# A graph kernel on one core: edges to the first 256 destination nodes taken from SBUF, the others gathered

## The chip, the cores and the metric

The kernel runs on one core of one Trainium2 chip. The time of a run is the device time of that core in microseconds (us), here the median of three runs. Beside the runs there is one profiled execution, from which every duration comes. A core has five engines, each with its own queue that it works off in order: TensorE (PE, its weight loads are shown as PEld), VectorE (DVE), ScalarE (ACT), GpSimd (POOL) and SyncE (SP, which issues DMAs).

## The reference

There are 12500 nodes with 256 features and 200000 edges from `src` to `dst`. `src` is uniform; `dst` is 12500 times the square of a uniform number, so low nodes are hit far more often. The edges come sorted by `dst`.

```python
h = relu(layernorm(x));  e = h @ W_P_w + W_P_b + W_pos          # 12500 x 128
for each of 2 layers:                                            # 8 heads of 16
    q = e[src] @ qT;  k = e[dst] @ kT;  v = e[dst] @ vT          # one row per edge
    a = exp(clip(sum over a head of q * k, -10, 10))
    agg = segment_sum(a * v, src) / (segment_sum(a, src) + 1e-8)
    e = layernorm(agg + e) * ln_s + ln_b
x = x + e @ inv_w + inv_b
h = relu(layernorm(x))
x = x + segment_sum(edge_weight * (h @ w_nbr)[src], dst) + h @ w_own + bias
```

## The kernel before

Nodes are taken in 98 tiles of 128. An edge belongs to the tile of its `src` (in the two attention layers) or of its `dst` (in the neighbour sum at the end). Edges are laid out in columns of 128, one edge to a partition, and the columns of a tile follow one another, filled up with idle edges; in the code `MAIN` = 1616 columns hold all edges of the drawn inputs.

**Prelude.** `sort_edges` (L306) makes one 32-bit key of each edge, with the tile in the high bits, the place of `src` within its tile (or 128 for a filler) from bit 14 and `dst` below, counts the edges of each tile (`count_tiles`, L175, by one-hot planes that TensorE multiplies), adds fillers and sorts 128 x 2048 keys by a bitonic network on VectorE (`stage`, L267). It leaves `idx_a` (the `dst` of each edge), `place_a` (its place within the tile), the same places as rows in DRAM (`place_d`) and the tile of each column (`near_d`). Beside it `embed` (L543) makes the first embedding of every tile and `project` (L510) its q, which stays in SBUF, and its rows of k and v, 256 floats a node, which go to the DRAM table `tkv`. `plan_as_they_come` (L394) lays out the neighbour sum. The flags in `bad` choose, at L1111, between a general arm and `short_arm` (L1007), which the drawn inputs take.

**Attention.** `short_attention` (L825) goes over 202 steps of `K2` = 8 columns for each layer. In its steady order, for step t:
- `gathers(t+2)`: 8 indirect DMAs from GpSimd's queue (L848, issued at L581) fetch the k and v rows of 8 columns into `kvg`, which has three buffers. An indirect DMA takes one column: 128 rows of 1 KB.
- `spread_hot(t+2)`: ScalarE turns the places, which a DMA has spread over the partitions (`load`, L837), into transposed one-hot matrices by Abs and Relu (L855, L857).
- `take_q(t+1)`: TensorE multiplies them with the tile's q (L871), which gives each edge its q in PSUM. The tile is a register that `registers` loads.
- `logits(t)`: VectorE multiplies q and k (L879), sums each head (L881), clips (L882). `exps(t)`: ScalarE's Exp (L887) and a copy (L888).
- `edge_hot(t+1)`: the one-hot matrix of places (L893). `weighted(t)`: VectorE scales v (L898).
- `sums(t)`: TensorE multiplies the one-hot matrix with the weights and the scaled v (L910) and adds up two steps in one PSUM tile `ps` of two windows, cleared by a product with zeros (L903); `add_window` (L590) adds it to `acc` every second step.

The order inside this arm is written out by hand (`manual_schedule`); L918 to L948 give it. Node work of finished tiles is hung into it at slots: `attended_later` (L685) divides, adds and normalises, `next_layer` (L733) projects for layer two, and after layer two `neighbour_rows` (L758) makes the rows of `h @ w_nbr` and the own part. The step from which a tile may be finished comes from `ends_by` (L80), a bound on the columns used by the first tiles (16.5 a tile).

**Neighbours.** `short_neighbours` (L950) gathers 1616 columns of the table `th` and sums them with weighted one-hot matrices (L604). `results` stores the output.

Of the kernel before, what the change touches and what calls it, by code (L numbers as in the profile page):

```python
# [33 lines left out]
P = 128  # L35
# [18 lines left out]

CG = -(-NCOL // P)
# [10 lines left out]
BASE = 1 << 29  # L66
TILE_MASK = 127 << 22
LAST = BASE | NT << 22 | P << 14

HI, LO, CB = -(-NT // 8), 8, 9  # L70
HPARTS = 6
# [4 lines left out]
MOST = RC - 1  # L76
SLOPE, SLACK = 16.5, 8.0


def ends_by(t):  # L80
    return min(MAIN, int(SLOPE * (t + 1) + SLACK))
# [3 lines left out]
def gnn_kernel(ctx, tc, x, src, dst, edge_weight, wp_w, wp_b, w_pos, q1, k1, v1, ln1_s, ln1_b,  # L85
# [23 lines left out]
    part_neg = const.tile([P, 1], F32, name="part_neg")  # L109
    nc.vector.tensor_scalar(part_neg, part_f, -1.0, None, op0=OP.mult)  # L110
    bad = const.tile([P, 4], F32, name="bad")
# [26 lines left out]
    def qkv_of(pool, layer):  # L138
        t = pool.tile([P, 3, D], F32, name=f"qkv{layer}")
        for j, w in enumerate(((q1, k1, v1), (q2, k2, v2))[layer]):  # L140
# [3 lines left out]
    qkv_sb = [None, qkv_of(const, 1)]  # L144
    ln_sb = [(row(s, D, f"lns{i}"), row(b, D, f"lnb{i}"))
             for i, (s, b) in enumerate(((ln1_s, ln1_b), (ln2_s, ln2_b)))]
# [7 lines left out]

    near_d = [dram.tile([1, CG * P // RC, RN], I32, name=f"near{i}") for i in range(2)]

# [4 lines left out]
    idx_a = keep.tile([P, NCOL], I32, name="idx_a")  # L161

    place_a = keep.tile([P, NCOL], F32, name="place_a")
# [11 lines left out]
    def count_tiles(pool, psum, key, shift, room):  # L175


        cross = psum.tile([P, CB * LO], F32, name="small", tag="turned")
        nb = HC // CB

        planes = [r.bitcast(BF16)[:, 0:n * HC] for r, n in zip(room, (HI, LO))]
        for part in range(HPARTS):
            have = min(HC, EC - part * HC)
            ti = pool.tile([P, HC], I32, name="ti")
            if have < HC:
                nc.vector.memset(ti, 127)
            nc.vector.tensor_scalar(ti[:, 0:have], key[:, part * HC:part * HC + have], shift, 127,
                                    op0=OP.logical_shift_right, op1=OP.bitwise_and)
            for n, down, mask, hot in ((HI, 3, 15, planes[0]), (LO, 0, 7, planes[1])):
                digit = pool.tile([P, HC], I32, name="digit")  # L190
                nc.vector.tensor_scalar(digit, ti, down, mask, op0=OP.logical_shift_right, op1=OP.bitwise_and)
                short = pool.tile([P, HC], BF16, name="short")
                nc.vector.tensor_copy(short, digit)
                for i in range(n):
                    nc.vector.tensor_scalar(hot[:, i * HC:(i + 1) * HC], short, float(i), None, op0=OP.is_equal)
            for c in range(nb):
                nc.tensor.matmul(cross[:CB * HI], planes[0][:, c::nb], planes[1][:, c::nb],
                                 start=(part == 0 and c == 0), stop=(part == HPARTS - 1 and c == nb - 1))
            yield
# [3 lines left out]
        own = pool.tile([P, LO, CB], F32, name="own")  # L203
        nc.vector.tensor_mul(own[:CB * HI], cross[:CB * HI].rearrange("p (l c) -> p l c", c=CB),
                             same[:CB * HI, None, :].to_broadcast([CB * HI, LO, CB]))
        sums = pool.tile([P, LO], F32, name="sums")
        nc.vector.tensor_reduce(sums[:CB * HI], own[:CB * HI], AX.X, OP.add)
# [5 lines left out]
        by_tile = psum.tile([P, CB * LO], F32, name="small", tag="turned")  # L213
        nc.tensor.matmul(by_tile[:HI * LO, 0:LO], wide[:CB * HI].rearrange("p h l -> p (h l)"), sums[:CB * HI],
                         start=True, stop=True)

        low = pool.tile([P, 1], I32, name="low")
        nc.vector.tensor_scalar(low, part_i, LO - 1, None, op0=OP.bitwise_and)
        low_f = pool.tile([P, 1], F32, name="low_f")
        nc.vector.tensor_copy(low_f, low)  # L220
        pick = pool.tile([P, LO], F32, name="pick")
        nc.vector.tensor_scalar(pick, iota_f[:, 0:LO], low_f, None, op0=OP.is_equal)
        nc.vector.tensor_mul(pick[:HI * LO], pick[:HI * LO], by_tile[:HI * LO, 0:LO])
        n = pool.tile([P, 1], F32, name="n")
        nc.vector.memset(n, 0.0)
        nc.vector.tensor_reduce(n[:HI * LO], pick[:HI * LO], AX.X, OP.add)
        return n

    def columns_of(pool, psum, n, which):
# [5 lines left out]
        nc.vector.tensor_scalar(cols, ni, float(LEAST), None, op0=OP.max)  # L235
# [4 lines left out]
        nc.vector.tensor_scalar(bad[:NT, which:which + 1], ends[:NT], float(MAIN), None, op0=OP.is_gt)  # L240
        if which == 0:
            by = pool.tile([P, 1], F32, name="by")
            nc.vector.tensor_scalar(by, part_f, SLOPE, SLOPE + SLACK, op0=OP.mult, op1=OP.add)
            late = pool.tile([P, 1], F32, name="late")
            nc.vector.tensor_tensor(late[:NT], ends[:NT], by[:NT], op=OP.is_gt)
            few = pool.tile([P, 1], F32, name="few")
            nc.vector.tensor_scalar(few[:NT - 1], cols[:NT - 1], float(MOST), None, op0=OP.is_lt)
            nc.vector.tensor_tensor(late[:NT - 1], late[:NT - 1], few[:NT - 1], op=OP.add)
            nc.vector.tensor_copy(bad[:NT, 3:4], late[:NT])
        return cols, ends  # L250

    def fillers(pool, dest, wide, n, cols):

        want = pool.tile([P, 1], F32, name="want")
        nc.vector.tensor_scalar(want, cols, float(P), n, op0=OP.mult, op1=OP.subtract)
        mask = wide.bitcast(I32)[:, 0:FILL]
        for k in range(LEAST):
            left = pool.tile([P, 1], F32, name="left")
            nc.vector.tensor_scalar(left, want, float(k * P), None, op0=OP.subtract)
            nc.vector.tensor_scalar(mask[:, k * P:(k + 1) * P], iota_f, left, None, op0=OP.is_lt)  # L260
        key = pool.tile([P, 1], I32, name="fkey")
        nc.vector.tensor_scalar(key, part_i, 22, None, op0=OP.logical_shift_left)
        nc.vector.tensor_scalar(key, key, BASE | P << 14, None, op0=OP.bitwise_or)
        nc.vector.memset(dest, LAST)
        nc.vector.copy_predicated(dest[:NT], mask[:NT], key[:NT].to_broadcast([NT, FILL]))
# [40 lines left out]
    def sort_edges(pool, psum, mine, other, weight=None):  # L306

        which = 0 if weight is None else 1
# [12 lines left out]
        yield  # L321
        nc.vector.tensor_tensor(ai[:, 0:EC], ai[:, 0:EC], bi[:, 0:EC], op=OP.bitwise_or)
# [4 lines left out]
        n = yield from count_tiles(pool, psum, ai[:, 0:EC], 22, (b, w))  # L327
        cols, _ = columns_of(pool, psum, n, which)
        fillers(pool, ai[:, FILL0:W], b, n, cols)
# [40 lines left out]
        yield from turned(psum, a, b, NCOL)  # L370
        ai, bi = a.bitcast(I32)[:, 0:NCOL], b.bitcast(I32)[:, 0:NCOL]
        if w is None:
            nc.vector.tensor_scalar(idx_a, bi, (1 << 14) - 1, None, op0=OP.bitwise_and)
            nc.vector.tensor_scalar(wi[:, 0:NCOL], bi, 14, 255, op0=OP.logical_shift_right, op1=OP.bitwise_and)
            nc.vector.tensor_copy(place_a, wi[:, 0:NCOL])
# [13 lines left out]
        nc.vector.tensor_scalar(ai[0:1], ai[0:1], NT - 1, None, op0=OP.min)  # L389
        near = near_d[which][:, 0:NCOL // RC, :]  # L390
# [3 lines left out]
    def plan_as_they_come(pool, psum):  # L394
# [15 lines left out]
        cols, ends = columns_of(pool, psum, n, 1)  # L410
# [201 lines left out]
    def attention_edges(pool, psum, q, acc, layer, chunks):  # L612
        for ch in chunks:
# [8 lines left out]
            for g in range(0, RC, K2):  # L622
                kvg = pool.tile([P, K2, 2 * D], F32, name="kvg", bufs=3)
                for k in range(K2):
                    c = ch * RC + g + k
                    gather(kvg[:, k, :], tkv[layer], idx_a[:, c:c + 1])

                far = pool.tile([P, K2 * P], BF16, name="far", bufs=2)
                nc.scalar.activation(far, spread[:, g * P:(g + K2) * P], AF.Abs, bias=part_neg)
# [55 lines left out]
    def attended_later(node, slots, acc, t0, t, layer):  # L685
# [4 lines left out]
        def load():  # L690
            e = tiles["e"] = node.tile([P, D], F32, name="e", bufs=4)
            nc.sync.dma_start(e[:n], emb_d[layer][t * P:t * P + n, :])

        def whole():
# [5 lines left out]
            y = node.tile([P, D], F32, name="y")  # L700
# [23 lines left out]
        def copy_e():  # L724
            et = tiles["et"] = node.tile([P, P], F32, name="et")
# [32 lines left out]
    def neighbour_rows(node, slots, weights, acc, acc1, t0, t):  # L758

        n = rows_of(t)  # L760
        inv_sb, w2_sb, inv_b_row, bias_row = weights
# [6 lines left out]
        def outwards():  # L768
            po = tiles["po"] = slots["psum"].tile([P, 4 * P], F32, name="out_e", tag="n1")
            nc.tensor.matmul(po[:n, 0:GD], tiles["et"][:, :n], inv_sb, start=True, stop=False)  # L770
            nc.tensor.matmul(po[:n, 0:GD], ones[0:1, :n], inv_b_row, start=False, stop=True)
# [15 lines left out]
        def centred():  # L787
            c = tiles["c"] = node.tile([P, GD], F32, name="c")
# [7 lines left out]
        def relu():  # L796
            ht = tiles["ht"] = node.tile([P, 2, P], F32, name="ht")
            nc.scalar.activation(ht[:, :, :n], tiles["pt2"][:, 0:2, :n], AF.Relu)

        def both():  # L800
# [4 lines left out]
            nc.tensor.matmul(pz[:n, GD:], ones[0:1, :n], bias_row, start=False, stop=True)  # L805
# [13 lines left out]
        for when, slot, emit in ((t0 + 1, "load", load), (t0 + 2, "pe2", outwards), (t0 + 3, "dve", whole),  # L819
                                 (t0 + 4, "act2", root), (t0 + 4, "dve", normal), (t0 + 5, "act", centred),  # L820
                                 (t0 + 5, "pe", turn_c), (t0 + 5, "act2", relu), (t0 + 5, "pe2", both),
                                 (t0 + 6, "act", rows), (t0 + 6, "dve", own), (t0 + 6, "store", store)):
            slots["at"].setdefault((when, slot), []).append(emit)

    def short_attention(pool, psum, q, acc, layer, after):  # L825

        steps = MAIN // K2
        of = {}
        slots = {"at": {}, "psum": psum}
        iota_p = psum.tile([P, P], F32, name="iota_p")  # L830
        nc.scalar.copy(iota_p, iota_f)
        before = -1
        for t in range(NT):
            before = max(before + 2, 2 * ((ends_by(t) - 1) // RC) + 2)
            after(slots, before, t)

        def load(ch):  # L837
# [307 lines left out]
```

## Time and profile before

| | us |
|---|---|
| three runs, median | 7039.77 |
| lowest and highest | 7039.05 and 7043.17 |
| the profiled execution, its own time | 7038.34 |
| its span, first to last instruction | 7036.6 |
| first gather of layer one | 837.45 |
| first gather of layer two | 2885.40 |
| first gather of the neighbour sum | 4956.99 |

Over the span the engines are busy for 4943 us (PE), 3359 (PEld), 4029 (DVE), 2311 (ACT) and 4652 us (POOL), and the mean granted TensorE clock is 0.723. A line of a group names the source line, the engine, the operation, output and inputs with shapes, and the count; after the bar stand busy time, the mean of one in ns, and how long the engine was idle just before these instructions with what ended that wait. In the rows by stretch the counts in brackets are instructions. A share of busy time is an average over stages, so the stages are read one by one.

### The profile page before, as it was taken

The numbers are of one execution on the slowest core, as the hardware profiler recorded it, in microseconds if no ns is written. First come the engines' busy times: TensorE is split into PE (matmuls) and PEld (weight loads), VectorE is DVE, ScalarE is ACT, GpSimd is POOL, SyncE is SP. The second block draws the span as 40 slices with busy tenths as digits, with TensorE's granted clock in tenths as the row PEclk, the third lists the DMA queues.
The fourth block names the chain that finished last, engine by engine and source line by source line (L and its number), as shares of the span: only waits on it lengthen the run. The fifth ranks groups of instructions, "written<-read, shape, count | busy, mean of one in ns | idle before, by whom it ended". The sixth has DMA issues, their size and how long they took to land.

```text
span 7036.6 us, 75317 instructions
## 1 busy us (share of the span) xinstructions
PE 4942.9 (70%) x19889; PEld 3359.3 (48%) x19889; DVE 4028.9 (57%) x9062; ACT 2311.0 (33%) x3864; POOL 4651.5 (66%) x4906
## 2 busy tenths in 40 slices
PE   4465555555555555577777777777888899888996
PEld 3254355555555555555655655565333334333432
DVE  3988466666666666577777777766333333333332
ACT  1233344444444444365666566655000000000000
POOL 0000477777777777677777777776677777777775
PEclk6556678878788788788888888888656555565555
DMA  1111444444444444444454444444333333333335
GB/s 59 38 41 46 120 143 145 142 145 146 144 144 144 145 144 146 124 147 147 148 150 148 146 148 149 149 145 129 93 105 105 105 105 105 105 105 105 105 105 148
DMA packets 429480, 864.26 MB, mean 123 GB/s; under 512 B 101103, under 2 KB 246416, under 8 KB 429024
## 3 DMA queue, kind: packets, MB, share of 16 engines
q0 software_dynamic: 234144, 638.70, 31.7%
q1 hardware_dynamic: 176618, 210.19, 9.0%
q10 hardware_dynamic: 18310, 10.47, 0.5%
q8 instruction: 190, 3.11, 0.2%
q14 instruction: 218, 1.79, 0.1%
HBM read 791.57 MB, written 69.80 MB: 122 GB/s over the span
## 4 chain that ended last, share of the span: by engine, by line
POOL 37%; issue 17%; DMA 16%; DVE 11%; PE 6%; ACT 0%; DVEq 0%; POOLq 0%; ACTq 0%; SPq 0%
POOL kvg L581 37%; DMA kvg<-tkv,idx_a 14%; DVE att L881 5%; PE ps L910 4%; DVE kvg L879 3%; DMA kvg<-th,plan 2%; DVE kvg L898 2%; DVE hot L893 1%; PE ps L604 1%; PE qe L871 1%; PE out_c L803 0%; DVE att L882 0%; DMA rows<-come,begin 0%; PE out_e L743 0%; DVE acc L592 0%
## 5 line engine op out<-in xcount | busy, mean ns | idle before, releaser
L581 POOL DMA_INDIRECT kvg<-tkv,idx_a x3232 | 3058.9, 946 | 1021.4 <-issue 808.1
L581 POOL DMA_INDIRECT kvg<-th,plan x1616 | 1535.4, 950 | 542.6 <-issue 478.9
L604 PE MATMUL ps<-kvg,hot 128*128 128x256 f32 x3232 | 1710.3, 652 | 223.0 <-DMA kvg<-th,plan 196.9
L910 PE MATMUL ps<-kvg,hot 128*128 128x136 f32 x6464 | 1282.4, 375 | 652.1 <-DVE kvg L898 651.8
L910 PEld LDWEIGHTS ps<-kvg,hot 128*128 128x128 f32 x6464 | 1177.0, 271 | 840.6 <-DVE kvg L898 840.6
L604 PEld LDWEIGHTS ps<-kvg,hot 128*128 128x128 f32 x3232 | 757.2, 287 | 1006.7 <-DMA kvg<-th,plan 941.8
L879 DVE TENSOR_TENSOR kvg<-qe,kvg 128x512 f32<-128x512 f32 x808 | 558.4, 691 | 1110.8 <-DMA kvg<-tkv,idx_a 1006.0
L974 DVE TENSOR_SCALAR hot<-iota_f,place_a,plan 128x128 f32<-128x128 f32 x1616 | 434.0, 363 | 1320.9 <-PE ps L604 1317.4
L871 PEld LDWEIGHTS qe<-q,hot_t 128*128 128x128 f32 x6464 | 829.9, 206 | 136.6 <-issue 100.6
L871 PE MATMUL qe<-q,hot_t 128*128 x6464 | 865.6, 291 | 28.7 <-DMA kvg<-tkv,idx_a 20.5
L903 PE MATMUL ps<-none_row,none 1*128 1x136 bf16 x202 | 48.6, 241 | 741.6 <-DVE acc L592 736.7
L898 DVE TENSOR_TENSOR kvg<-ex,kvg 128x1024 f32<-128x1024 f32 x404 | 492.1, 1218 | 78.3 <-ACT kvg L888 77.7
L893 DVE TENSOR_TENSOR hot<-iota_p,place_a 128x1024 f32<-128x1024 f32 x404 | 491.8, 1217 | 26.0 <-DMA kvg<-tkv,idx_a 17.8
L881 DVE TENSOR_REDUCE att<-kvg 128x64 f32<-128x1024 f32 x404 | 493.0, 1220 | 13.7
L857 ACT ACTIVATE hot_t<-far,ones 128x1024 f32<-128x1024 bf16 x404 | 464.0, 1149 | 15.2 <-PE qe L871 2.0
L855 ACT ACTIVATE far<-spread,part_neg 128x1024 bf16<-128x1024 bf16 x404 | 462.1, 1144 | 12.8 <-DMA spread<-place_d 12.7
L421 POOL IOTA room<- 128x1920 int32 x1 | 1.7, 1732 | 626.1 <-DVE room L414 626.1
L887 ACT ACTIVATE ex<-att 128x64 f32<-128x64 f32 x404 | 93.4, 231 | 967.6 <-DVE att L882 966.4
L887 ACT ACT_TABLE_LOAD x286 | 366.9, 1283 | 21.8 <-DVE att L882 16.8
L481 ACT ACT_TABLE_LOAD x287 | 368.2, 1283 | 14.2 <-DMA wp_sb<-in_L_gnn_W_P_w_dram 9.2
L903 PEld LDWEIGHTS <-none 1*128 1x128 bf16 x202 | 19.0, 94 | 672.9 <-DVE acc L592 671.2
L592 DVE TENSOR_TENSOR acc<-acc,ps 128x256 f32 (+1 forms) x606 | 253.3, 418 | 4.5 <-PE ps L910 4.5
(178 smaller groups left out, 4297.1 us busy)
## 6 DMA issues: line engine op xcount, KB each, us to landing
spread<-place_d SPq DMA_DIRECT2D x202, 512.0 KB
kvg<-tkv,idx_a POOLq DMA_INDIRECT x3232
kvg<-th,plan POOLq DMA_INDIRECT x1616
xt<-in_x_dram SPq DMA_DIRECT2D x194, 128.0 KB
emb<-e SPq DMA_DIRECT2D x194, 64.0 KB
tkv<-kv_out SPq DMA_DIRECT2D x97, 128.0 KB
e<-emb SPq DMA_DIRECT2D x194, 64.0 KB
tkv<-out_rows SPq DMA_DIRECT2D x97, 128.0 KB
```

The source lines that it names most:

```text
L581: nc.gpsimd.indirect_dma_start(out=dest, out_offset=None, in_=table, in_offset=bass.IndirectOffsetOnAxis(ap=idx, axis=0))
L604: nc.tensor.matmul(ps[:, bass.ds(at, 1), :].rearrange("p a b -> p (a b)") if k else ps[:, 0, :], hot[k], rows[k], start=False, stop=(k == ...
L855: nc.scalar.activation(far, spread[:, g * P:(g + K2) * P], AF.Abs, bias=part_neg)
L857: nc.scalar.activation(hot_t.rearrange("p k e -> p (k e)"), far, AF.Relu, bias=ones[:, 0:1], scale=-1.0)
L871: nc.tensor.matmul(qe[:, k, :], of["hot_t", i][:, k0 + k, :], q[:, bass.ds(of["tiles", i][k0 + k], 1), :], start=True, stop=True)
L879: nc.vector.tensor_mul(kk, qe, kk)
L881: nc.vector.tensor_reduce(att, kvg[:, :, 0:D].rearrange("p k (h d) -> p k h d", d=HD), AX.X, OP.add)
L887: nc.scalar.activation(ex, of["att", i].rearrange("p (k h) -> p k h", h=HEAD), AF.Exp)
L893: nc.vector.tensor_tensor(hot, iota_p[:, None, :].to_broadcast([P, K2, P]), place_a[:, i * K2:(i + 1) * K2, None].to_broadcast([P, K2, P]) ...
L898: nc.vector.tensor_mul(vv, of.pop(("ex", i))[:, :, :, None].to_broadcast([P, K2, HEAD, HD]), vv)
L910: nc.tensor.matmul(ps[:, 0, :] if first else ps[:, bass.ds(at, 1), :].rearrange("p a b -> p (a b)"), of["hot", i][:, k, :], of["kvg", i][: ...
L974: nc.vector.tensor_scalar(hot[:, k, :], iota_f, plan[1][:, c:c + 1], plan[2][:, c:c + 1], op0=OP.is_equal, op1=OP.mult)
```

## The change

Destinations are split at node 256. For every tile of `src` the edges to these 256 nodes (near) get 3 columns of their own and are no longer gathered; all others (far) keep the old way, in 1392 columns, taken in 174 steps of 8.

- A key bit `FAR_BIT` above the tile makes the first sort put all near edges, by tile, ahead of the far ones. `count_tiles` counts both kinds at once (16 low planes for 8, and 7 parts for 6), `look_at` sets the flags, fillers are two columns near and one far. The first sort also stores the destinations of the near columns (`other_d`). The flags take the short arm if the far columns of the first tiles stay under a bound of 14.25 a tile, each tile but the last has 7 far columns at least, and each has 128 to 384 near edges.
- At the start of each layer `kvn` loads the k and v rows of the 256 nodes into SBUF. `seen`, once a tile, spreads places and destinations, makes their one-hot matrices on ScalarE, and takes q (3 products), k and v (6 each, two blocks of 128 nodes) for its 384 edges on TensorE; then logits, Exp, weighting, one-hot matrix, 3 products and one addition to `acc`.
- A step's window is cleared by a VectorE memset in PSUM and added once a step. `edge_hot` stands behind `weighted` in the order; `ex` lies in one PSUM tile with `iota_p`; `qe` has 4 buffers for 3; several node buffers become single.
- The two bias products of `neighbour_rows` become bf16 products with three rows that add up to the bias.
- Weights and layer rows load at the start of the short arm; indices and places of the neighbour sum are loaded into `idx_a` and `place_a` in the tail of layer two, the weights after it. The general arm makes its own sort.

```diff
+SB, SEEN, STEP, FAR = 2, 3, 8, 1392
+MOST = STEP - 1
+SLOPE, SLACK = 14.25, 4.0
-HPARTS = 6
+HPARTS = 7
...
+        if short:
+            nc.vector.tensor_scalar(wi[:, 0:EC], bi[:, 0:EC], float(SB * P), float(FAR_BIT), op0=OP.is_ge, op1=OP.mult)
+            nc.vector.tensor_tensor(ai[:, 0:EC], ai[:, 0:EC], wi[:, 0:EC], op=OP.bitwise_or)
...
-            nc.tensor.matmul(po[:n, 0:GD], ones[0:1, :n], inv_b_row, start=False, stop=True)
+            nc.tensor.matmul(po[:n, 0:GD], ones_b[:, :n], rows3[:, 0, :], start=False, stop=True)
...
+        kvn = pool.tile([P, SB, 2 * D], F32, name="kvn")
+        nc.sync.dma_start(kvn, tkv[layer][0:SB * P, :].rearrange("(b p) d -> p b d", p=P))
+        def seen(t, t0):
...
+            def take():
+                hot_t = its["hot_t"]
+                for key in "kqv":
+                    to = its[key] = psum.tile([P, K, D], F32, name="qe", tag="qe", bufs=4)
+                    for k in range(SEEN):
+                        if key == "q":
+                            nc.tensor.matmul(to[:, k, :], hot_t[:, 0, k, :], q[:, t, :], start=True, stop=True)
+                            continue
+                        half = slice(0, D) if key == "k" else slice(D, 2 * D)
+                        for b in range(SB):
+                            nc.tensor.matmul(to[:, k, :], hot_t[:, 1 + b, k, :], kvn[:, b, half],
+                                             start=(b == 0), stop=(b == SB - 1))
+            def logits():
+                kk = pool.tile([P, SEEN, D], F32, name="kk")
+                nc.vector.tensor_copy(kk, its["k"][:, 0:SEEN, :])
+                nc.vector.tensor_mul(kk, its["q"][:, 0:SEEN, :], kk)
...
+            for when, slot, emit in ((t0 - 4, "load", load), (t0 - 2, "act2", spread_hot), (t0 - 1, "pe0", take),
+                                     (t0 - 1, "dve0", logits), (t0 - 1, "exps", exps), (t0 - 1, "dve2", weighted),
+                                     (t0 - 1, "sums", sums), (t0, "first", add)):
+                put(when, slot, emit)
...
-            before = max(before + 2, 2 * ((ends_by(t) - 1) // RC) + 2)
+            before = max(before + 1, (ends_by(t) - 1) // STEP + 1)
+            seen(t, before)
...
+        def room_for(i):
+            ps = of["ps", i] = psum.tile([P, 2, AW], F32, name="ps")
+            nc.vector.memset(ps[:, 1, :], 0.0)
...
             do(spread_hot, t + 2)
+            other_work("act")
+            other_work("first")
+            do(logits, t)
+            other_work("pe0")
+            other_work("dve0")
             do(take_q, t + 1)
+            other_work("dve1")
             do(exps, t)
+            other_work("exps")
+            other_work("pe")
+            do(adds, t - 1)
+            do(room_for, t)
+            do(weighted, t)
             do(edge_hot, t + 1)
+            other_work("dve2")
+            other_work("act2")
+            do(registers, t + 2)
             do(sums, t)
+            other_work("sums")
+            other_work("pe2")
+            other_work("dve")
+            other_work("store")
             t += 1
```

## The prediction

> **What bounds the kernel now.** I first cut the execution at the first and last gather of each stage, which the timeline shows, and asked for busy time per stretch: prelude up to 837.45 us, layer one, a gap, layer two, a gap, neighbour sum, stores. Columns: stretch, its length, busy time of TensorE, weight loads, VectorE, ScalarE and GpSimd, then the granted TensorE clock, DMA share, GB/s.
>
> ```profile
> 837.45:2859.40 2021.95, 1157.45 (x6828) 1059.37 (x6829) 1291.01 (x2360) 864.66 (x1376) 1530.00 (x1616) 0.80 0.49 145
> 2859.40:2885.40 26.00, 11.85 (x33) 6.76 (x32) 9.84 (x31) 5.48 (x18) 0.00 (x1) 0.57 0.25 49
> 2885.40:4906.30 2020.90, 1484.08 (x7754) 1177.27 (x7755) 1429.63 (x2916) 1196.01 (x1748) 1528.91 (x1616) 0.83 0.49 147
> 4906.30:4957.00 50.70, 34.62 (x87) 16.74 (x86) 19.30 (x68) 10.86 (x28) 0.02 (x2) 0.63 0.16 41
> 4957.00:6984.30 2027.30, 1805.36 (x3630) 794.59 (x3629) 698.74 (x2419) 0.00 (x0) 1535.34 (x1616) 0.59 0.36 105
> ```
>
> Three stages with very different work on VectorE and TensorE take the same time: 1616 gathers in 2021, 2021 and 2027 us, 1.25 us each. GpSimd looks 76% busy, but its timeline shows no hole:
>
> ```profile
> 2886.64 0.95 POOL L581 DMA_INDIRECT kvg<-tkv,idx_a  x1 [0.30 <-issue]
> 2887.89 0.95 POOL L581 DMA_INDIRECT kvg<-tkv,idx_a  x1 [0.30 <-issue]
> ```
>
> 0.95 us of gather and 0.30 us of issue, again and again: 10.0 us for a step of 8 columns. The chain that ended last and the groups agree:
>
> ```profile
> POOL 37%; issue 17%; DMA 16%; DVE 11%; PE 6%; ACT 0%; DVEq 0%; POOLq 0%; ACTq 0%; SPq 0%
> ...
> L581 POOL DMA_INDIRECT kvg<-tkv,idx_a x3232 | 3058.9, 946 | 1021.4 <-issue 808.1
> ...
> L879 DVE TENSOR_TENSOR kvg<-qe,kvg 128x512 f32<-128x512 f32 x808 | 558.4, 691 | 1110.8 <-DMA kvg<-tkv,idx_a 1006.0
> L893 DVE TENSOR_TENSOR hot<-iota_p,place_a 128x1024 f32<-128x1024 f32 x404 | 491.8, 1217 | 26.0 <-DMA kvg<-tkv,idx_a 17.8
> ```
>
> VectorE's large idle time ends on gathered data: it has slack, but how much is the question, since the change moves work to it. Per step it is busy 6.4 us in layer one (1291/202) and 7.1 in layer two, TensorE 5.7 and 7.3, ScalarE 4.3 and 5.9.
>
> **Gathers removed.** Columns per layer fall from 1616 to 1392; counting the drawn edges gives 1385 far columns, so 1392 holds them, and each tile's near edges (170 to 335) fit 3 columns. 224 x 1.251 = 280 us less gathering per layer. The neighbour sum keeps 1616: no change there (TensorE's fourth qe buffer is idle cover, since gathers pace it). GpSimd's new floor is 174 steps x 10.01 = 1741 us a layer. The gain stands only where the other engines stay under 10.0 us a step.
>
> **VectorE in the new step.** Durations from the groups. Main work: L879 2 x 0.69, L881 1.22, L882 0.21, L893 1.22, L898 1.22, the window addition once a step and no longer every second 0.43, a memset of 136 in place of TensorE's zero product 0.17 (memset of acc, L705): 5.85 us. There are 98/174 = 0.563 tiles a step, 0.485 before. A tile's node work sums to 2.73 us in layer one (L698 to L718) and 4.51 in layer two (also L775 to L785, L475, L477, L813). The new near set has seven instructions a tile: copy, product, reduction, weighting and one-hot of 384 elements, clip of 24, addition of 136. No row has 384 elements; between 256 (L775, 0.41) and 512 (L879, 0.69) I take 0.55: 5 x 0.55 + 0.17 + 0.29 = 3.2 us. Bounds: 2.3 (all at 0.41 or, for the copy, half of it) to 3.9 (all at 0.69).
> The same sum for the kernel before gives 6.78 and 7.65 us where 6.4 and 7.1 were measured, since instructions overlap at their ends: factor 0.94. So after: layer one (5.85 + 0.563 x 5.9) x 0.94 = 8.6 us, layer two (5.85 + 0.563 x 7.7) x 0.94 = 9.6 us (9.1 to 10.0 by the bounds). Layer one stays covered. Layer two has 0.4 us left.
>
> **TensorE.** Measured 5.7 and 7.3 us a step. Of that 1.5 and 5.3 us a tile are node work (timeline: turn_e 0.3, out_e 1.2; in layer two outwards 0.75 + bias 0.75, turn_c 0.4, out_c 2.4 + bias 0.7), so the main part is 4.9, less 0.12 for the zero product. The near set adds 15 products of 128 columns and 3 of 136. The timeline has 8 products of L871 in 2.05 us: 15 x 0.256 = 3.8; three of L910 by 3.6/8 are 1.35, without register arithmetic nearer 0.8: 4.8 us a tile. The two bias products become bf16 single passes: 1.45 us becomes about 0.75 (L600: 0.37 each). Layer one 4.8 + 0.563 x 6.3 = 8.3; layer two 4.8 + 0.563 x 9.4 = 10.1 us, at the old clock.
> Here a rule is weighed. The neighbour stage is TensorE's busiest (89%) and has the lowest clock, 0.59. By that row more work would bring a lower clock: 10.1 x 0.83/0.59 = 14.2 us. The Trainium skill says the opposite (TensorE: Matmul & The Clock Gate, "What's actually happening"): half rate is the default and sustained activity releases it; and (Trainium Kernel Development and Optimization, opening section) matmul busy time is a poor measure, weight-load share a better one. By weight loads the trace agrees with the rule: shares 39%, 52%, 58% have clocks 0.59, 0.80, 0.83; in the neighbour stage TensorE waits for data before each product. The new layer two has longer runs of products, so I take a clock near 0.9 and 9.3 us; at full clock 8.4.
>
> **ScalarE.** The near set: Abs of 768 and 384, Relu of 1152 and a small Exp. From L855 (1024: 1.14) and 256 elements (0.38), about 0.9 + 0.5 + 1.3 + 0.2 = 2.9 us a tile. Layer two: 5.9 + 0.078 x 7.3 (more tiles a step, 7.3 us of node work each with its table loads) + 0.563 x 2.9 = 8.1 us: under 10, cover kept.
>
> **Waits added.** VectorE and ScalarE work in order. In a step with a near set VectorE's copy of k waits for TensorE's products, which stand behind the last step's sums and out_c; queued behind that copy are this step's weighting, hence TensorE's sums, hence the release of kvg. The addition of a near sum waits for TensorE too. Laying two steps of layer two side by side (TensorE sums ready at 4.9 us, done 8.2, outwards 9.2, k and q 11.5, against VectorE ready for q at 11.4) gives waits of 0 to 1 us. L876-L882's existing waits for TensorE and ScalarE are 0.3 us a step. I put 0.6 us a step in layer two; bounds 0.2 and 2.5, the length of out_c. So layer two 10.2 us x 174 = 1775; layer one 8.6 + 0.6, under the gathers: 1742. Of kvg's three buffers one is slack (some 5 us), which smooths heavy steps.
> edge_hot, which used to cover ScalarE's Exp before the weighting, is moved behind it; the additions and the memset (0.6 us) or a near set take its place, against 0.5 us for Exp and copy: nothing counted, 0.2 us a step if late, within the 0.6.
>
> **Prelude.** VectorE is 87% busy between 200 and 690 us, so sorting is on the path. The first count has 7 parts for 6 and 16 low planes for 8: 203 comparisons for 126 at 0.13 to 0.15 us, +8 us, with five more shifts and casts, +3; two instructions for the far bit +2.7 (L318, L320); destinations for the near rows +2.4 (L366, L368); other small ones +1. Sum 17 us, from 0 (70 to 200 us has VectorE half idle) to 30 (each part also waits for its products, 10 us a part).
> The layer rows' loads move to the start of the short arm: 7 more DMA issues of 0.45 us on ScalarE's queue and 3 that wait for VectorE, about 9 us before its first activation, under the first gathers' 10 us and their landing. SP's queue gets two loads of 96 KB a tile, 0.35 us to issue; it has gaps of microseconds. Nothing. The gap between layers (26 us) +2 for kvn; the gap before the neighbours (50.7 us) -5: one step fewer in the tail, indices and places loaded earlier, the weights' load in their place.
>
> **Sum.** Span 7036.6 + 17 - 280 (layer one) - 246 (layer two, 2021 - 1775) + 2 - 5 = 6525; the profiled run lies 1.4 us under the median and 1.7 over its span, so 6528 for the median.
>
> **Rivals.**
> - Gathers bind both layers and the prelude hides its additions: 7036.6 - 280 - 280 - 3 + 5 = 6479, about 6482. For it: VectorE's sum is below 10. Against: 96% busy in order. Chance 0.13.
> - The loop through TensorE binds: each of 98 near sets costs 2.5 us in both layers. Layer one 174 x 8.6 + 245 = 1741, no loss; layer two 174 x 9.6 + 245 = 1915: 6525 + 140 = 6665, 6668 for the median. For it: in-order queues and single buffers (near one-hots, ps). Chance 0.27, from 6590 to 6720.
> - Slower: TensorE becomes the bound at the neighbour stage's clock: 8.3 x 0.80/0.59 = 11.3 us and 14.2 us a step give 1966 + 2471, against 4043 before: 7036.6 + 394 + 14 = 7445. It turns slower where both layers' steps average 11.6 us. Against: the clock rose from layer one to two. Chance 0.04.
> - The counts don't fit and the other arm runs, with another sort: far slower. The count above speaks against it: 0.01.
> - Forecast 0.55, its own range 6482 to 6590.
>
> The range 6465 to 6700 takes in the first two and the bounds; little can lie below it, since 1741 us a layer is GpSimd's floor and only the prelude and the gaps are left to shorten. Faster by over 0.2% (about what a measurement of this kernel can tell from no change): 0.94; within 0.2%: 0.01; slower: 0.05.
>
> **What would show it.** 2784 gathers of tkv at 946 ns; first gather near 855 us; layer one at 10.0 us a step with issue as the only idle; layer two at 10.0 to 10.4 with some gathers waiting for TensorE's release of kvg; VectorE 86% and 95% busy; a clock above 0.83 in layer two. Wrong would be: layer one over 10.2 a step (waits worse than 1.4 us), gathers longer beside more vector work, or a clock below 0.8.

## The result and the profile after

The changed kernel takes 6927.18 us (median of 4 runs, 6921.42 to 6939.50) against 7039.96 for the kernel before beside it: ratio 0.9841, 95% interval 0.9824 to 0.9858. It is faster by 1.6%, clear of the noise, but only 113 of the 512 us forecast came, and the time lies outside the range of 6465 to 6700. The profiled execution took 6921.42 us with a span of 6919.6. Four of the kernels below were first run where the kernel before took 8383 us beside them, for a cause that the record does not show; those first runs (early_whole 7718, early_whole_add 7700, no_near_two 7717, before_own_behind 8710 us) are not compared, and the runs with `_b` behind the name repeat them.

The same cut by stretch as before the change (stretch, length, busy time of TensorE, weight loads, VectorE, ScalarE, GpSimd, then granted clock, DMA share, GB/s), from the first to the last gather of each stage:

```profile
867.05:2614.30 1747.25, 1292.65 (x9282) 1189.12 (x9283) 1479.22 (x3110) 1079.61 (x1650) 1318.68 (x1392) 0.92 0.56 158
2614.30:2651.60 37.30, 22.32 (x110) 17.36 (x109) 19.00 (x54) 11.00 (x24) 0.01 (x1) 0.73 0.20 35
2651.60:4772.77 2121.17, 1608.57 (x9974) 1376.88 (x9974) 1623.02 (x3637) 1296.54 (x1928) 1316.04 (x1392) 0.88 0.47 132
4772.77:4842.10 69.33, 47.44 (x200) 28.52 (x201) 37.63 (x112) 24.37 (x48) 0.01 (x1) 0.77 0.22 61
4842.10:6867.40 2025.30, 1800.21 (x3630) 784.36 (x3629) 698.28 (x2419) 0.00 (x0) 1533.34 (x1616) 0.60 0.36 105
```

Layer one came down to the gathers' pace, 10.04 us a step. Layer two, with the same 1392 gathers, did not: 2121 us, 12.19 a step, 100 us more than with 1616 gathers. And no engine is full in it: per step TensorE 9.24, VectorE 9.33, ScalarE 7.45 us of 12.19. So it looks as if a loop of waits sets the pace and not anyone's work; the experiments below test this. The chain that ended last, by engine, and the groups say the same: GpSimd's share fell from 37% to 23%, TensorE's rose from 6% to 27%, and gathers, no longer than before at 946 ns, stood idle for something other than issue for 1281.7 - 712.1 = 570 us, where it was 213 before (waits at stage starts among them).

```profile
PE 27%; POOL 23%; issue 15%; DVE 14%; DMA 6%; DVEq 1%; ACT 0%; POOLq 0%; SPq 0%; ACTq 0%
...
L641 POOL DMA_INDIRECT kvg<-tkv,idx_a x2784 | 2634.7, 946 | 1281.7 <-issue 712.1
...
L1044 PE MATMUL ps<-kvg,hot 128*128 128x136 f32 x5568 | 1009.2, 353 | 868.4 <-DVE kvg L1036 591.4
```

The waits within layer two (who waited, for whom, us in total, times, longest):

```profile
POOL kvg L641 <- PE ps L1044: 395.5, 136, 7.8
...
PE ps L1044 <- DVE kvg L1036: 309.0, 118, 7.3
...
DVE kk L937 <- PE qe L931: 129.3, 87, 3.9
DVE q L873 <- PE turn_e L782: 86.5, 52, 1.8
DVE q L873 <- PE qe L1005: 72.3, 40, 2.1
```

Read from the top it is a ring: gathers wait for TensorE's sums to release `kvg`, sums wait for VectorE's weighting (L1036), and VectorE stands 159 us at L873 for TensorE, besides 129 at the copy of k (L937). L873 is `own`, the node's own part, which the prediction charged as work and not as a wait. The chain through one such step, in order of time (start, us, what):

```profile
3408.36 3.97 PE ps L1044 x16
3412.33 2.71 PE out_c L863 x4
3415.04 0.21 PE out_c L865
3415.25 1.53 PE qe L931 x12
3416.78 0.67 PE qe L927 x6
3417.45 1.34 PE qe L931 x12
3418.80 1.79 PE qe L1005 x16
3420.58 0.12 PE turn_e L782
3420.71 0.14 DVE q L873
...
3420.90 0.29 DVE acc L873
...
3421.21 0.45 DVE acc L652
...
3421.92 1.13 DVE kvg L1036
...
3423.09 2.74 PE ps L1044 x16
```

From one step's sums to the next it takes 14.73 us. `own`'s input, `out_c`, is complete at 3415.25, yet `own` starts only at 3420.7: after the near set's products (L931, L927) and after `take_q` of the next step (L1005). VectorE stands idle twice on the way, once for the near set's k and once at `own`:

```profile
3416.82 0.56 DVE L937 COPY kk<-qe 128x384 f32<-128x384 f32 x1 [1.85 <-PE qe L931]
...
3420.69 0.29 DVE L873 TENSOR_TENSOR q<-out_c,xt 128x128 f32<-128x128 f32 x1 [1.84 <-PE turn_e L782]
```

The reason for the second wait is in the program. `own` adds into `acc1[0]`, which is `q`; `take_q` reads `q` at a tile that a register names, so a write to any tile of `q` issued after it waits for all of its products. (The profile names `turn_e` in 52 of the 92 cases, but the order issues `turn_e` behind `own`. In 91 of the 92 cases, whichever is named, `own` starts 0.11 us after the last product of `take_q`.) And the change moved `own`, from the end of the step to right behind `take_q` and ahead of the weighting:

```diff
-                                 (t0 + 6, "act", rows), (t0 + 6, "dve", own), (t0 + 6, "store", store)):
+                                 (t0 + 6, "act", rows), (t0 + 6, "dve1", own), (t0 + 6, "store", store)):
```

### The profile page after: what moved, and what is told of

It is laid out like the page before. It is cut to its first block, busy times and chain, and to the rows that moved or that the text cites. A ratio compares the mean times of both kernels' runs of the same rounds, so it can differ in the third digit from the quotient of the medians.

```text
span 6919.6 us, 87145 instructions
## 1 busy us (share of the span) xinstructions
PE 5246.1 (76%) x24757; PEld 3718.6 (54%) x24757; DVE 4457.9 (64%) x10731; ACT 2648.1 (38%) x4345; POOL 4225.4 (61%) x4458
## 3 DMA queue, kind: packets, MB, share of 16 engines
q0 software_dynamic: 212640, 579.95, 29.6%
## 4 chain that ended last, share of the span: by engine, by line
PE 27%; POOL 23%; issue 15%; DVE 14%; DMA 6%; DVEq 1%; ACT 0%; POOLq 0%; SPq 0%; ACTq 0%
POOL kvg L641 23%; PE ps L1044 10%; PE qe L931 4%; PE qe L1005 4%; DMA kvg<-tkv,idx_a 4%; DVE kvg L1036 3%; PE out_c L863 3%; DMA kvg<-th,idx_a 2%; DVE att L1015 2%; PE qe L961 2%; DVE kvg L1013 1%; DVE acc L652 1%; PE qe L927 1%; PE ps L664 1%; DVE hot L1027 1%
## 5 line engine op out<-in xcount | busy, mean ns | idle before, releaser
L641 POOL DMA_INDIRECT kvg<-tkv,idx_a x2784 | 2634.7, 946 | 1281.7 <-issue 712.1
L641 POOL DMA_INDIRECT kvg<-th,idx_a x1616 | 1533.4, 949 | 561.3 <-issue 476.7
L1044 PE MATMUL ps<-kvg,hot 128*128 128x136 f32 x5568 | 1009.2, 353 | 868.4 <-DVE kvg L1036 591.4
L1044 PEld LDWEIGHTS ps<-kvg,hot 128*128 128x128 f32 x5568 | 928.7, 251 | 941.8 <-DVE kvg L1036 524.8
L664 PEld LDWEIGHTS ps<-kvg,hot 128*128 128x128 f32 x3232 | 747.0, 284 | 1017.6 <-DMA kvg<-th,idx_a 967.0
L1005 PE MATMUL qe<-q,hot_t 128*128 x5568 | 706.3, 280 | 82.1 <-ACT hot_t L995 39.4
L1005 PEld LDWEIGHTS qe<-q,hot_t 128*128 128x128 f32 x5568 | 661.8, 195 | 124.2 <-issue 44.9
L931 PE MATMUL qe<-kvn,hot_s 128*128 128x128 f32 x4704 | 609.8, 280 | 6.9 <-ACT hot_s L919 6.3
L931 PEld LDWEIGHTS qe<-kvn,hot_s 128*128 128x128 f32 x4704 | 572.8, 195 | 40.6 <-ACT hot_s L919 8.9
L1036 DVE TENSOR_TENSOR kvg<-still,kvg 128x1024 f32<-128x1024 f32 x348 | 421.6, 1211 | 5.3 <-ACT kvg L1021 4.5
L1027 DVE TENSOR_TENSOR hot<-still,place_a 128x1024 f32<-128x1024 f32 x348 | 422.0, 1213 | 0.0
```

Source lines behind the costliest of these rows:

```text
L641: nc.gpsimd.indirect_dma_start(out=dest, out_offset=None, in_=table, in_offset=bass.IndirectOffsetOnAxis(ap=idx, axis=0))
L664: nc.tensor.matmul(ps[:, bass.ds(at, 1), :].rearrange("p a b -> p (a b)") if k else ps[:, 0, :], hot[k], rows[k], start=False, stop=(k == ...
L931: nc.tensor.matmul(to[:, k, :], hot_t[:, 1 + b, k, :], kvn[:, b, half], start=(b == 0), stop=(b == SB - 1))
L1005: nc.tensor.matmul(qe[:, k, :], of["hot_t", i][:, k0 + k, :], q[:, bass.ds(of["tiles", i][k0 + k], 1), :], start=True, stop=True)
L1027: nc.vector.tensor_tensor(hot, iota_p[:, None, :].to_broadcast([P, STEP, P]), place_a[:, c:c + STEP, None].to_broadcast([P, STEP, P]), op= ...
L1036: nc.vector.tensor_mul(vv, ex[:, :, :, None].to_broadcast([P, STEP, HEAD, HD]), vv)
```

## The experiments

The theory: `own`'s wait for `take_q`, ahead of the weighting, closes the ring, and it costs that much only where the near set's products stand on TensorE between `out_c` and `take_q`. The second half of it did not hold in full, as shift_early shows. The rivals: sheer work on TensorE and VectorE; VectorE's copy of k waiting for TensorE in any case; the move costing by itself.

| kernel | layer two, us | waits of its gathers beyond issue | time, us |
|---|---|---|---|
| after | 2121.2 | 382 | 6927 |
| own_late | 1960.9 | 220 | 6755 |
| own_add_late | 1937.2 | 197 | 6733 |
| own_aside | 1904.5 | 164 | 6700 |
| own_early | 1865.4 | 125 | 6665 (one run) |
| early_whole_b | 1859.2 | 120 | 6649 |
| early_whole_add_b | 1842.8 | 103 | 6641 |
| early_half | 1843.1 | 103 | 6646 (one run) |
| no_near_two_b | 1741.2 | 0 | 6530 (one run) |
| shift_one | 1949.1 | 210 | 6747 |
| shift_early | 1793.2 | 53 | 6593 |
| shift_all | 1799.3 | 60 | 6600 |

The third column adds up what the gaps between the gathers of layer two have over the 0.30 us of issue. Layer one is 1745 to 1749 us in all of them. The times of the profiled executions differ from the medians by up to 14 us, and the start of layer one by up to 12; the comparisons therefore rest on the length of layer two in one profile of each kernel. Runs of one kernel differ by 4 to 20 us, so a difference of that size between two kernels shows little.

**own_late.** `own` behind the weighting:

```diff
-... (t0 + 6, "dve1", own), ...
+... (t0 + 6, "own", own), ...
...
             other_work("exps")
-            other_work("pe")
             do(adds, t - 1)
             do(room_for, t)
             do(weighted, t)
+            other_work("own")
+            other_work("pe")
             do(edge_hot, t + 1)
```

> The kernel after, with own (the two additions of L873, which write a tile of q) moved from right behind take_q to right behind the weighting (TensorE's turns are issued behind it too; TensorE's own order stays). Theory 'own waits for take_q': 130 of the 380 us that gathers wait in layer two go, between 80 and 300; layer two 2121 to about 1990 us, the whole near 6800. Rival 'sheer work' (TensorE and VectorE each need over 9 us a step): no change, within 20 us. Rival 'near logits wait for k anyway' (VectorE stands at the copy of k until TensorE is through sums and out_c, wherever own is): under 50 us. Layer one stays at 1747 in all.

Layer two 160 us shorter, the time 6755. The theory's size; neither rival allows it. That it gains less than the next two may come from what its chain shows in the step at 3427 us: `own`, then turn_c and the Relu that follows it, stand between weighting and sums, 1.4 us.

**own_aside.** Same place, same work, without the one dependence:

```diff
+            aside = node.tile([P, D], F32, name="aside", bufs=1)
-                nc.vector.tensor_add(to[:n, t, :], tiles["pz"]...
+                nc.vector.tensor_add(to[:n, t, :] if h else aside[:n], tiles["pz"]...
```

> The kernel after, with own in its place right behind take_q and all its instructions, but its first addition writes to a tile that nothing reads instead of q's (so the first 128 output columns lack the node's own term and hold q under the neighbour sum). Only the wait of own's first half for take_q goes. Theory 'own waits for take_q': as own_late, near 6800 (100 to 300 us faster than after). Rivals 'sheer work' and 'near logits wait for k anyway': 6927, within 40.

Layer two is 217 us shorter with every instruction still in its place, and VectorE's work is nearly the same (1612.42 us, 1623.02 in after):

```profile
2659.77:4564.22 1904.45, 1529.48 (x9975) 1285.53 (x9976) 1612.42 (x3640) 1295.48 (x1928) 1316.91 (x1392) 0.91 0.52 147
```

This is the cleanest evidence that it is the wait and not the work. TensorE's busy time for the same products fell too, from 1608.57 to 1529.48 us, while the clock rose from 0.88 to 0.91: part of the gain may be a faster TensorE, which these runs don't separate from the shorter waits.

**own_early.** `own` ahead of the products that it used to wait for:

```diff
-... (t0 + 6, "dve1", own), ...
+... (t0 + 6, "own", own), ...
...
             do(logits, t)
+            other_work("own")
             other_work("pe0")
```

> The kernel after, with own right behind logits, ahead of the near set's products and of take_q. VectorE now stands at own until out_c is done, which the copy of k has to wait for anyway, and take_q waits for own. Theory 'own waits for take_q': 60 to 200 us faster than after, less than own_late. Rivals: no change within 40, or slower since take_q now waits for VectorE.

256 us: more than the 60 to 200 expected, and the best place of the three, where less than own_late was expected. Its waits in layer two, the same rows as above:

```profile
POOL kvg L641 <- PE ps L1044: 153.4, 109, 5.7
...
DVE kk L937 <- PE qe L931: 58.5, 48, 1.5
```

Even the copy of k waits less than half as long as in after; that TensorE comes earlier because the ring is shorter fits this, but wasn't tested by itself.

**own_add_late, early_whole_b, early_whole_add_b.** The other two additions for which VectorE waits ahead of the weighting, the near sum (L964) and the x rows of `whole` (L835), moved behind it too: the near sum on own_late; `whole`, then both, on own_early:

```diff
-... (t0, "first", add)...
+... (t0, "add", add)...
-... (t0 + 3, "dve1", whole), ...
+... (t0 + 3, "late", whole), ...
...
             do(weighted, t)
+            other_work("add")
+            do(take_q, t + 1)
+            other_work("late")
+            other_work("pe")
```

> own_late, and the addition of the near sum (L964) moved too, from ahead of logits to right behind the weighting, with take_q issued behind it. VectorE's logits no longer wait for TensorE's near sums (65 us of waits in layer two). Theory: 30 to 100 us faster than own_late, near 6740. Rival 'sheer work': no change against after.

> early_whole again, since in its first run the kernel before itself took 8383 us. own ahead of the near set's products (own_early), and whole of the node rows (L835) moved from ahead of the weighting to behind it. Theory that every product of TensorE that VectorE waits for ahead of the weighting lengthens the loop: 30 to 90 us faster than own_early's 6665, near 6610. Rival that what is left is the near set's work itself: within 20 us of 6665.

> early_whole_add again: early_whole, and the near sum's addition behind the weighting as well, with take_q issued behind that. Theory: another 10 to 40 us, total near 6580, layer two near 1780. Rival: no further gain, or a loss of up to 30.

The near sum's place gave 24 us of layer two on own_late (30 to 100 expected) and 16 on early_whole_b, `whole`'s gave 6; all three on own_early came to 6641, not to 6580. Only the first of these differences is clear of the spread of runs. The theory in its broad form, that every such wait lengthens the ring, was too generous: for `whole` the rival was right.

**no_near_two_b and before_own_behind_b.** The two halves of the theory alone: `own` behind `take_q` without near sets, and in the kernel before.

```diff
-            seen(t, before)
+            if layer == 0:
+                seen(t, before)
```

> no_near_two again: the kernel after with own in its place behind take_q, but layer two's near sets left out. Theory: own's wait hurts only since the near set's products stand between out_c and take_q, so layer two falls to the gathers' pace, 1741 to 1800 us, total 6550 to 6600. Rival 'the move of own costs by itself': layer two stays over 1900 us.

```diff
-... (t0 + 6, "dve", own), ...
+... (t0 + 6, "dve1", own), ...
...
+            scheduled(slots["at"], t, "dve1")
             do(exps, t)
             do(edge_hot, t + 1)
```

> before_own_behind again: the kernel before with own moved to where the change puts it, between logits and weighting, behind take_q. Theory that own's place costs only together with the near set's products: 7040 within 20 us. Rival 'the move costs by itself': 50 to 250 us slower. (In the first run both kernels were over 1300 us longer than here, and this one 3.9% slower than before.)

Without near sets layer two runs at the gathers' pace with `own` where the change put it, though VectorE still waits there for some 90 us. In the row by stretch VectorE and TensorE have 388 and 520 us to spare:

```profile
2658.36:4399.57 1741.21, 1221.60 (x6572) 984.45 (x6573) 1353.69 (x2992) 1018.56 (x1552) 1317.44 (x1392) 0.84 0.52 150
```

And the kernel before with the move takes 7039.94 against 7037.84: ratio 1.0002, interval 0.9994 to 1.0011. So the place of `own` costs nothing without near sets; with them it costs 256 us. The near sets do cost something by themselves: with `own` ahead of them (own_early) layer two still lies 124 us over the gathers' pace.

**shift_one, shift_early, shift_all.** Why together? Four tiles are 4 x 14.25 = 57 columns, 7.1 steps, so `own` at `t0` + 6 of one tile falls on `t0` - 1, the near set's step, of the tile four later: by the code's constants in 82 of 98 cases. One step later it would be 21. The traces agree: near products stand between `out_c` and `own` in 80 of the 92 cases within layer two of after, and in 20 of 91 in shift_one.

```diff
-... (t0 + 5, "pe2", both),
-    (t0 + 6, "act", rows), (t0 + 6, "dve1", own), (t0 + 6, "store", store)...
+... (t0 + 6, "pe2", both),
+    (t0 + 7, "act", rows), (t0 + 7, "dve1", own), (t0 + 7, "store", store)...
```

> The kernel after with out_c, own, rows and their store one step later (t0 + 6 and t0 + 7), own still right behind take_q; xt with a fourth buffer and ht with a second. By the schedule's constants own (t0 + 6) falls on a step that takes a near set (t0 - 1 of a later tile) for 82 of 98 tiles, at t0 + 7 for 21. Theory that own's wait costs where out_c, the near set's 15 products and take_q stand ahead of it in one step, some 3 us each time: 61 fewer, about 190 us faster than after, near 6740 (6680 to 6800). Rival that own's wait for take_q costs in any step: no change, 6927 within 40.

> shift_one with own ahead of the near set's products and take_q as in own_early. Theory that what is left in own_early (10.7 us a step in layer two) is out_c and the near set's products in one step of TensorE: 30 to 90 us under own_early's 6665, near 6600. Rival that it is the near set's own length, in whichever step out_c stands: 6665 within 25.

> shift_early with whole and the near sum's addition behind the weighting, as in early_whole_add: every product that VectorE waits for ahead of the weighting is taken away but the near set's own k and q. Theory: near 6570, layer two 1750 to 1790. Rival: as early_whole_add, 6641 within 25.

shift_one still has `own` behind `take_q` and gains 172 us, as forecast: a step in which `out_c`, a near set and `own` meet is dear, by 2.8 us for each of the 61 meetings fewer. `out_c` moves along with `own`, and `xt` and `ht` have a buffer more, so what each of them gives isn't separated. And the place of `own` is dear beyond these meetings: at `own` VectorE still waits 125 us,

```profile
DVE q L873 <- PE qe L1005: 98.4, 71, 2.2
...
DVE q L873 <- PE turn_e L782: 26.6, 20, 1.8
```

and shift_early, which moves `own` ahead as well, gains another 156 us, more than the 21 meetings left can hold at that price (59 us). That the near sets use up the slack of the steps around them too would explain it, but wasn't tested.

shift_early, with both edits, is the best version: 6593.40 us (6587.60 to 6595.94), 0.9366 of the kernel before (0.9351 to 0.9380). Its layer two takes 10.31 us a step, the gathers wait 53 us in all, and the clock rises further:

```profile
2655.41:4448.60 1793.19, 1436.61 (x9986) 1202.31 (x9986) 1611.62 (x3642) 1292.61 (x1927) 1316.38 (x1392) 0.98 0.55 156
```

shift_all adds nothing to it, against both expectations (6570, or 6641 as its rival): the moves that gave 22 us on own_early are worth nothing once `out_c` is out of the way.

**early_half.** The near set's length on TensorE:

```diff
+                        blocks = SB if layer == 0 else 1
-                        for b in range(SB):
+                        for b in range(blocks):
```

> own_early with layer two's near sets taking k and v from one block of 128 rows instead of two, 9 products for 15 (the output lacks the edges of nodes 128 to 255 in layer two; all else stays). If TensorE's length in a step with a near set sets what is left: 98 times 1.5 us at most, 60 to 120 us under own_early's 6665. If VectorE's and ScalarE's near instructions set it: within 25 us.

Layer two lost 22 us where TensorE's length would have given 60 to 120, though TensorE was busy for 106 us less (1413.79 for 1520.27). In own_early the six products are not most of what is left; `out_c` in the same step is more (72 us, shift_early). What makes up the last 52 us above the gathers' pace wasn't tried. VectorE is then busy for 90% (1611.62 of 1793.19 us), so for this rest sheer work, uneven from step to step, is not ruled out.

## Why the prediction was wrong, point by point

- **What bounds before, and the gathers removed: right.** 946 ns before and after; layer one 1747 us, 1742 forecast.
- **The work: right.** Per step of layer two VectorE 9.33 (9.6), TensorE 9.24 (9.3 at a clock of 0.9), ScalarE 7.45 (8.1). The shares forecast for VectorE, 86% and 95%, came out as 85% and 77%, since the step grew and not the work. (The near set's terms on TensorE, 3.8 and 0.8, make 4.6 us a tile and not the 4.8 that was entered: 0.1 us a step.)
- **The clock: right, its size in part by luck.** 0.92 and 0.88 in the two layers (about 0.9 forecast for layer two), 0.60 in the neighbour sum. But 0.88 belongs to a step of 12.19 us; at 10.31 us a step, near the 10.2 forecast, shift_early had 0.98 and 8.26 us of TensorE, near what the forecast gave for the full clock (8.4). The rule taken from the Trainium skill (TensorE: Matmul & The Clock Gate, "What's actually happening"), that sustained activity releases the rate, held against the neighbour row; for the same products the clock went up as layer two got shorter: 0.88, 0.91, 0.92, 0.98 at 2121, 1904, 1865 and 1793 us. With fewer products and no waits (no_near_two_b) it was 0.84. The share of weight loads orders these only roughly: 39% has 0.60, 57% has 0.84, 65% has 0.88, but 68% (layer one) has 0.92 and 67% (shift_early) 0.98; the page that the prediction cites for this share speaks of the distance to the roofline, not of the clock. The slower rival was wrong at this step.
- **The waits added: the step that failed.** "I put 0.6 us a step in layer two; bounds 0.2 and 2.5, the length of out_c." By that sum the step of 12.19 us, less VectorE's 9.33 of work, holds 2.86 us in which VectorE stands, over the bound too. Gathers waited 382 us, 2.2 a step, where the forecast of 10.2 leaves 0.2. The list of waits named the copy of k and the near sum; it left out `own`, which the change moved from behind the sums to ahead of the weighting. Of the 380 us above the floor, 256 go with its place, 72 more with `out_c` standing in a near set's step, 52 remain (with the shift first, it is 172 and then 156). The two steps that were laid side by side had `out_c` in them but not what `own` waits for, and not that the schedule puts the two together 82 times in 98. Why one place of `own` costs 256 us where VectorE itself waits 159 us at it is not taken apart further.
- **The range.** The range didn't carry even the prediction's own bound of 2.5 us a step: 174 x (9.6 + 2.5) = 2105 us for layer two is a time of 6858. The rival "the loop through TensorE binds" came nearest: it had the loop and the in-order queues, but not `own`, and charged 2.5 us to each of 98 near sets over VectorE's work, where layer two shows (2121 - 1623) / 98 = 5.1. Layer one, which has no `own`, showed no loss, as it said.
- **Prelude: undersized.** The first gather came 29.6 us later; 17 was put in and 30 the bound. The first count was costed on VectorE, but TensorE paces it, with the embedding beside it: it is busy for 57.93 of 63.10 us before and for 73.45 of 78.70 after, at 391 and 434 ns a product of the count, and VectorE waits for it.

```profile
L197 PE MATMUL small<-keys,keys 128*117 128x72 bf16 x174 | 38.1, 391 | 23.5 <-DVE keys L195 23.5
...
L195 DVE TENSOR_SCALAR keys<-short 128x261 bf16<-128x261 bf16 x107 | 15.7, 224 | 23.0 <-PE small L197 23.0
```

```profile
L220 PE MATMUL small<-keys,keys 128*117 128x144 bf16 x175 | 45.9, 434 | 2.9 <-DVE keys L218 2.9
...
L218 DVE TENSOR_SCALAR keys<-short 128x225 bf16<-128x225 bf16 x177 | 23.8, 216 | 26.4 <-PE small L220 26.4
```

  (Groups within the first count of the kernel before, then of after.) The count lasts 15.6 us longer; the other 14 us of the delay were not taken apart.
- **Gaps: undersized.** Between the layers 37.3 us (28 forecast), with near sets in layer two or without; before the neighbours 69.3 (46), but 50.0 in no_near_two_b, so 19 us of it go with layer two's near sets.

The miss adds up: prelude 12.6, layer one 5, gap 9, layer two 346, gap 24, neighbours -2: 395 us, and the span is 6919.6 - 6525 = 394.6 over the forecast.

## What to carry to other kernels

When a change moves an instruction in an in-order queue, list what it waits for at its new place, the dependence through a tile read by register index included, and what is queued behind it, even if its own work is 0.3 us. Then lay the schedule's periods over each other: two pieces that each fit in a step can be dear where they fall on the same one; here 61 meetings fewer gave 172 us. Where no engine is busy for more than 77% and the step is yet far longer than anyone's work, look for a ring of waits, and move its cheapest member first.

## What the runs showed of the hardware

An indirect gather of 128 rows of 1 KB took 946 to 950 ns and 0.30 us to the next in both kernels, beside very different work on the other engines: 1.25 us each is the floor of both layers and of the neighbour sum. For the same products in layer two the granted clock rose from 0.88 to 0.98 as the stage got shorter. In the first count a product with 144 columns took 434 ns where one with 72 had taken 391, at clocks of 0.66 and 0.58: with the clock counted in, an estimate from these four numbers, doubling the columns added a quarter.
